# Zero points of the second wave unpacked on chip, row tiles loaded two steps apart, first results stored sooner

## The chip, the cores and the metric

The kernel runs on one core of one Trainium2 chip. The metric is the device time of one execution in microseconds, the median of three runs. The profile shows one further execution; all times of single instructions below are counted from the start of its span.

## What is computed

The input `u` has 2 x 1024 rows of 1024 numbers, 2048 rows in all. The reference is a "macaron": half a feed-forward layer, a state-space convolution along the rows, and half a feed-forward layer again.

```python
x = x + 0.5 * ffn(layernorm(x))
x = x + s4(layernorm(x))
x = x + 0.5 * ffn(layernorm(x))

def ffn(x):                       # 1024 -> 2752 -> 1024
    h = silu(x @ Wg) * (x @ Wu)
    return h @ Wd
# every W is packed in 4 bits, in groups of 128 rows:
W = (w4 - (z4 + 1)) * scale       # z4 (the zero points) is packed as well

def s4(u):                        # one kernel K of length 1024 for all rows
    K = ifft(c * (k00 - k01 * (1 / (1 + k11)) * k10)).real
    return irfft(rfft(u, n=2L) * rfft(K, n=2L))[..., :L] + D * u
```

## The kernel before

**Jobs, stages, steps.** The rows are cut into four blocks of 512. Eight jobs (a block and one of its two feed-forward layers) follow one another, and each has an up stage and a down stage. An up stage has 64 steps: eight "waves" of columns (three pairs of gate and up tiles, 128 columns each, in the first five waves, two pairs in the last three), and in each wave the eight groups of 128 weight rows. A step with three pairs is 12 matmuls of 128x128 weights on 512 rows (L876): the six weight tiles meet the low halves (`xTl`) and the high halves (`xTh`) of the activations. Sums stay in PSUM for the eight steps of a wave; after each step every sum `pg` is multiplied by the ratio of two group scales, on ScalarE or VectorE (L834, L838). After the last step of a wave, ScalarE makes `g` (L912) and VectorE `hf` (L915) of each pair; that frees the pair's two PSUM banks for the next wave. There are eight banks in all. GpSimd then splits `hf` into two halves `h` (L920, L921). A down stage has 44 steps (two halves of the output, 22 groups each) of eight matmuls (L993) into sums `po`, at the end of which `y` is copied out (L834, L838), turned by VectorE (L1052), stored to `yz` (L1058), read back by rows as `yr` (L1063) and added to the block's rows `x` by GpSimd (L1068).

**Weights.** Job 0 makes the weights once. For wave w the packed words `raw` are loaded and shifted into `even` and `raw` (L654), zero points `z` are added (L658), signs are fixed (L661), the bytes are cast to bf16 by ScalarE (L698) and GpSimd (L700), stored to DRAM (`wq`, L706; L642 for the first wave), and each step then loads its tile `w_s` from there (L804). Waves are counted from 0 in the code, so the second wave is wave 1 and its first tile is `w_8`. The zero points of wave 0 are unpacked on chip from `zq_first` (L351 shifts, L360). For the later waves all zero points are unpacked into a table `ztab`, stored to `z_dram` by ScalarE's queue (L380) and loaded per wave by two DMAs on SyncE (L597, `fetch_zeros`).

**The convolution kernel.** In the up stage of job 1 the tables of the state-space part are worked out in 71 pieces spread over the steps (`s4_tables`, `S4_PIECES`). Near the end, VectorE writes the kernel `k` (L1305), GpSimd adds D to one element of it (L1306), SyncE stores it to `k_dram` (L1308) and reads it back as a table `s_rows` with one row shifted per partition (L1325), and TensorE flips it with two matmuls per half (L1330).

**Order.** Each engine runs its instructions in the order of the built program. That order is made by a scheduler, except where the kernel fixes it: `pinned(f, engines)` and `in_order_of_writing` keep what `f` writes behind what was written before on these engines. `at(hooks, s, f)` hangs `f` on step s (s + 0.5: in its middle). A piece of `s4_tables` is kept in order on VectorE alone; GpSimd's chores (`squared`, `most`: L934, L935, the watch over the size of `h`) are kept in order on GpSimd. SyncE issues nearly all DMAs, one after another, and waits at the head of its queue. DMAs that SyncE and ScalarE issue use eight semaphore lanes in turn, and a DMA waits until the earlier one on its lane has landed. At the end of a down stage, `load_x` puts four loads of 512 KB on SyncE (L174) at one step, and `results_out` hangs the turns and stores of the first half's results.

## Time and profile before

| | us |
|---|---|
| three runs | 1948.53, 1948.57, 1949.28 |
| median | 1948.57 |
| the profiled execution, its own time | 1951.13 |
| its span | 1949.1 |
| TensorE busy | 1916.2 (98%) |
| VectorE, ScalarE, GpSimd busy | 1537.9, 1449.7, 1195.3 |
| mean granted TensorE clock | 0.998 |

The profiled execution took 2.56 us more than the median, and 2.0 us of it lie outside the span. TensorE is busy nearly all the time, so a change gains or loses what it takes from, or adds to, TensorE's idle time, and the time in which TensorE runs at less than its clock. Idle times of the other engines count only where TensorE ends up waiting for them.

Some places on the time axis: first up-stage matmul of job 0 at 17.86, its step 8 (the first of the second wave) at 47.16, its down stage from 180.3, up stage of job 1 from 261.04.

### The profile page before, as it was taken

What the parts mean: (1) busy time and instruction counts of PE and PEld (TensorE: products, weight loads), DVE (VectorE), ACT (ScalarE), POOL (GpSimd) and SP (SyncE); (2) the same over time, 40 slices, a digit from 0 to 9 for tenths busy, and PEclk for the clock granted to TensorE, in tenths of its full rate; (3) what the DMA queues carried; (4) which work ended last, traced back from release to release, by engine and by line L of the source; (5) the groups of instructions that cost most, each with busy time, mean ns of one, the idle gap of its engine ahead of it and who ended that gap; (6) DMA issues with size and microseconds to landing.
All of it is one profiled execution on the core that took longest, in us unless ns stands there. A gap on an engine that the chain in (4) does not pass through costs nothing.

```text
span 1949.1 us, 28195 instructions
## 1 busy us (share of the span) xinstructions
PE 1916.2 (98%) x9154; PEld 919.6 (47%) x9154; DVE 1537.9 (79%) x2592; ACT 1449.7 (74%) x2308; POOL 1195.3 (61%) x1314
## 2 busy tenths in 40 slices
PE   6999989999999999999999999999999999999998
PEld 3444434474445544444444444456444564444443
DVE  8888867877877778877887878777877777787787
ACT  7888867738786587787777877874878757777776
POOL 4756959858866681696427960574924858345630
PEclk9999999999999999999999999999999999999999
DMA  6666773345635356644373625443465433663225
GB/s 206 206 201 211 207 239 100 105 126 154 200 110 139 98 149 183 207 123 106 99 239 121 156 72 153 143 118 112 114 195 152 121 101 111 181 197 97 73 70 178
DMA packets 393602, 286.23 MB, mean 147 GB/s; under 512 B 208205, under 2 KB 367254, under 8 KB 393446
## 3 DMA queue, kind: packets, MB, share of 16 engines
q1 hardware_dynamic: 391982, 281.83, 49.9%
q10 hardware_dynamic: 1272, 2.12, 0.3%
q8 instruction: 74, 1.21, 0.3%
q14 instruction: 82, 0.67, 0.1%
q0 software_dynamic: 192, 0.39, 0.1%
HBM read 211.30 MB, written 72.75 MB: 146 GB/s over the span
## 4 chain that ended last, share of the span: by engine, by line
PE 90%; POOL 3%; DVE 2%; DMA 2%; ACT 2%; issue 1%; SPq 0%; ACTq 0%; DVEq 0%; POOLq 0%
PE pg L876 54%; PE po L993 30%; PE pc L1377 4%; PE pb L1377 1%; DVE pg L838 1%; ACT pg L834 1%; POOL most L935 1%; POOL h L921 1%; POOL squared L934 1%; DMA yr<-yz 0%; DMA wd<-wdq 0%; DMA x<-in_L_attn_u_dram 0%; POOL x L1068 0%; DMA z<-z_dram 0%; POOL h L920 0%
## 5 line engine op out<-in xcount | busy, mean ns | idle before, releaser
L834 ACT ACTIVATE pg<-pg,rat 128x512 f32<-128x512 f32 x1356 | 843.1, 661 | 328.4 <-PE pg L876 325.0
L876 PEld LDWEIGHTS <-w 128*128 128x128 bf16 x5504 | 537.6, 98 | 665.6 <-issue 29.8
L838 DVE TENSOR_TENSOR pg<-pg,rat 128x512 f32<-128x512 f32 x1052 | 698.9, 692 | 187.6 <-PE pg L876 182.6
L876 PE MATMUL pg<-xTl,w 128*128 128x512 f16 x2752 | 701.0, 379 | 5.0 <-ACT pg L834 1.7
L876 PE MATMUL pg<-xTh,w 128*128 128x512 f16 x2752 | 698.5, 379 | 5.7 <-DVE pg L838 1.9
L993 PE MATMUL po<-h,wd 128*128 128x512 f16 x2680 | 585.6, 380 | 3.8 <-DMA wd<-wdq 3.1
L834 ACT ACTIVATE po<-po,ratd 128x512 f32<-128x512 f32 x708 | 452.0, 664 | 103.4 <-PE po L993 102.1
L838 DVE TENSOR_TENSOR po<-po,ratd 128x512 f32<-128x512 f32 x572 | 394.3, 693 | 97.6 <-PE po L993 95.9
L993 PEld LDWEIGHTS <-wd 128*128 128x128 bf16 x2740 | 267.8, 98 | 331.6 <-issue 8.9
L920 POOL CAST h<-hf 128x512 f16<-128x512 f32 x168 | 107.4, 641 | 226.1 <-DVE hf L915 225.8
L935 POOL TENSOR_TENSOR most<-most,squared 128x512 f32<-128x512 f32 (+1 forms) x176 | 223.8, 1272 | 8.5
L1068 POOL TENSOR_TENSOR x<-x,yr 128x512 f32<-128x512 f32 x56 | 70.9, 1265 | 236.4 <-DMA yr<-yz 234.1
L921 POOL TENSOR_TENSOR h<-hf,h 128x512 f16<-128x512 f32 x168 | 194.7, 1162 | 10.9
L934 POOL TENSOR_TENSOR squared<-h 128x512 f32<-128x512 f16 x168 | 176.1, 1048 | 4.9
L915 DVE SCALAR_TENSOR_TENSOR hf<-pg,rat,g 128x512 f32<-128x512 f32 x168 | 120.7, 744 | 34.3 <-ACT g L912 28.9
L912 ACT ACTIVATE g<-pg,rat 128x512 f32<-128x512 f32 x168 | 109.9, 685 | 18.8 <-PE pg L876 14.0
L272 POOL TENSOR_SCALAR x<-x,mv,r 128x512 f32<-128x512 f32 x56 | 117.2, 2096 | 0.3
L312 POOL TENSOR_TENSOR xTl<-turned,xTh 128x512 f16<-128x512 f32 x56 | 64.6, 1154 | 3.7
L191 DVE BATCH_NORM_STATS2 stats<-x 128x6 f32<-128x512 f32 x88 | 59.2, 679 | 0.1
L310 POOL CAST xTh<-turned 128x512 f16<-128x512 f32 x56 | 34.1, 609 | 28.2 <-DMA turned<-tz 27.8
L1052 DVE STREAM_TRANSPOSE y<-y 128x256 f32<-128x256 f32 x120 | 50.5, 426 | 0.0
L1371 POOL TENSOR_TENSOR sums<-st 128x384 f32<-128x384 f32 x16 | 15.9, 997 | 55.3 <-PE pb L1377 55.2
(226 smaller groups left out, 866.9 us busy)
## 6 DMA issues: line engine op xcount, KB each, us to landing
w<-wq SPq DMA_DIRECT2D x319, 192.0 KB
wd<-wdq SPq DMA_DIRECT2D x336, 128.0 KB
w<-wq SPq DMA_DIRECT2D x128, 128.0 KB
x<-in_L_attn_u_dram SPq DMA_DIRECT2D x30, 512.0 KB
yz<-y SPq DMA_DIRECT2D x60, 256.0 KB
yr<-yz SPq DMA_DIRECT2D x60, 256.0 KB
tz<-x SPq DMA_DIRECT2D x28, 512.0 KB
turned<-tz SPq DMA_DIRECT2D x112, 128.0 KB
```

Source lines behind the costliest of these rows:

```text
L272: nc.gpsimd.tensor_scalar(part, part, m, r, ALU.subtract, ALU.mult)
L834: nc.scalar.activation(dst, src, AF.Copy, scale=sc)
L838: nc.vector.tensor_tensor(dst, src, sc.to_broadcast(list(dst.shape)), ALU.mult)
L876: product = lambda: nc.tensor.matmul(p, weights, (lo, hi)[k][:, g, :], start=(g == 0 and not done), stop=(g == GK - 1 and done), skip_grou ...
L912: nc.scalar.activation(g, pg, AF.Silu, scale=rat[:, 2 * f, GK - 1 :])
L915: nc.vector.scalar_tensor_tensor(hf, pu, last, g, ALU.mult, ALU.mult)
L920: nc.gpsimd.tensor_copy(hi, hf)
L921: nc.gpsimd.tensor_tensor(lo, hf, hi, ALU.subtract)
L934: chores.append(lambda: nc.gpsimd.tensor_tensor(own, hi, hi, ALU.mult))
L935: chores.append(lambda: nc.gpsimd.tensor_tensor(total, total, own, ALU.add))
L993: nc.tensor.matmul(ps[c], w[:, bass.ts(c, P)], part, start=(f == 0 and k == 0), stop=(f == NF - 1), skip_group_check=True,)
L1377: nc.tensor.matmul(dst, lhsT, rhs, start=start, stop=stop, skip_group_check=True)
```

## The change

The zero points of the second wave are no longer taken from the table. Their packed words are loaded by two more DMAs at the start (`zq_first_1`, one on SyncE after `x_2`, one on ScalarE's queue after `x_3`) and unpacked on VectorE in nine pieces, four before the first turned column block, four after it and one in step 1; the eight zero-point pieces of the table, its last step and its store to `z_dram` move from the start to steps 3 to 4.5 of job 0. The two table loads for wave 1 are gone, those for wave 2 hang on step 5 and no longer on step 2. Shifts, additions and casts of wave 1 hang on earlier steps.

In the down stage of job 0 the four row tiles are loaded at steps 37, 39, 41 and 43, the last row tile to be normalized is turned a little sooner, and the first half's results are turned from step 27.5 on in half steps and stored at steps 33 and 34.

In the state-space part, two ScalarE operations of 1024 columns are cut in halves with pieces between them, two sign changes move from VectorE to GpSimd, and the count of pieces goes from 71 to 74.

```diff
-    def load_x(b, src):
-        x[b] = []
+    def load_row_tile(b, src, t):
+        if t == 0:
+            x[b] = []
+        xt = t4(f"x_{b}_{t}")
+        nc.sync.dma_start(xt, src[t])
+        x[b].append(xt)
...
     def fetch_zeros(w):
...
-        packed[w][1] = z
+        zeros_of[w] = z
...
-    def first_zero_words():
+    def first_zero_words(w):
...
-            nc.vector.tensor_tensor(both, both, z.bitcast(U16), ALU.add)
+            nc.vector.tensor_tensor(both, both, z().bitcast(U16), ALU.add)
...
-            steps = (0.5, 1, 2.5, 3, 3.5) if w == 1 else range(6)
+            steps = (0.5, 1, 1.5, 2, 2.5) if w == 1 else range(6)
...
-            copies = {1: (3, 3, 3.5, 3.5) + (3.5,) * 4, 2: (3, 3, 4, 4, 5.5, 5.5, 6, 6)}
+            copies = {1: (2, 2, 2.5, 2.5) + (3,) * 4, 2: (3, 3, 4, 4, 5.5, 5.5, 6, 6)}
...
-        nc.vector.tensor_scalar(neg, vec[:, 0, :], -1.0, None, ALU.mult)
+        nc.gpsimd.tensor_scalar(neg, vec[:, 0, :], -1.0, None, ALU.mult)
         yield
         dr = t4("s4_dr")
-        nc.scalar.activation(dr, cs, AF.Copy, scale=neg[:, 0:1])
         di = sn
-        nc.scalar.activation(di, sn, AF.Copy, scale=alpha)
-        yield
         halves = [slice(0, 512), slice(512, HID)]
+        for own in halves:
+            nc.scalar.activation(dr[:, own], cs[:, own], AF.Copy, scale=neg[:, 0:1])
+            yield
+            nc.scalar.activation(di[:, own], sn[:, own], AF.Copy, scale=alpha)
+            yield
...
-        nc.vector.tensor_scalar(se[:, 1, :], se[:, 1, :], -1.0, None, mul)
+        nc.gpsimd.tensor_scalar(se[:, 1, :], se[:, 1, :], -1.0, None, mul)
...
-    S4_PIECES = 71
+    S4_PIECES = 74
...
-                    (0, lambda: fetch_zeros(1)),
                     (0, lambda: ask(5)),
...
                     (1, lambda: fetch(2)),
-                    (2, lambda: fetch_zeros(2)),
                     (3, lambda: keep_rest(3, 0)),
+                    (5, lambda: fetch_zeros(2)),
...
+                at(up, 1, pinned(lambda: next(later["zeros"], None), ET.DVE))
                 first_weights(up, dn, at)
+                steps = [(up, s) for s in (3, 3, 3, 3.5, 3.5, 3.5, 4, 4, 4, 4.5)]
+                in_pieces(at, steps, lambda: zero_points_in_pieces(0, later["points"]))
...
-                        turn = ((10.5, 11, 11.5, 12), (17.5, 18, 18.5, 19), (19.5, 24, 24.5, 25), (25.5, 26, 27, 28))[t]
+                        turn = ((10.5, 11, 11.5, 12), (17.5, 18, 18.5, 19), (19.5, 24, 24.5, 25), (25.5, 26, 26.5, 27))[t]
...
-            at(dn, 35 if after else 21, pinned(lambda: load_x(b, rows_of(u, b) if k == 1 else saved(b)), ET.SP))
+            src = rows_of(u, b) if k == 1 else saved(b)
+            if j:
+                at(dn, 35 if after else 21, pinned(lambda src=src: load_x(b, src), ET.SP))
+            for t in range(NT) if j == 0 else ():
+                at(dn, 37 + 2 * t, pinned(lambda t=t, src=src: load_row_tile(b, src, t), ET.SP))
             if j == 0:
-                results_out(at, dn, 0, range(29, 37), (38, 38, 39, 39))
+                results_out(at, dn, 0, [27.5 + i / 2 for i in range(8)], (33, 33, 34, 34))
...
     def start():
-        zq = first_zero_words()
+        zq = first_zero_words(0)
...
             (nc.sync, nc.scalar)[t % 2].dma_start(x[0][t], src)
+        zq_1 = first_zero_words(1)
...
-        points = zero_points_in_pieces(0, zeros)
+        zi_1, z_1 = (t4(f"{a}_w1").bitcast(I32)[:, : width_of(1)] for a in ("zi", "z"))
+        zeros_of[1] = z_1
+        later["zeros"] = unpacked_zeros_in_pieces(z_1, zq_1, zi_1)
+        later["points"] = zeros
         for _ in range(4):
-            next(points)
+            next(later["zeros"])
         first_turn(0)
-        for _ in range(5):
-            next(points)
+        for _ in range(4):
+            next(later["zeros"])
...
-        for _ in points:
-            pass
```

More of the change, by code (lines that the diff above doesn't have):

```diff
@@ L168, in macaron_s4_kernel @@
     ln = {}
+    def load_row_tile(b, src, t):
[4 more added lines that the diff above has]
+        x[b].append(xt)
     def load_x(b, src):
-        x[b] = []
         for t in range(NT):
-            xt = t4(f"x_{b}_{t}")
-            nc.sync.dma_start(xt, src[t])
-            x[b].append(xt)
+            load_row_tile(b, src, t)
     def rows_of(dram, b):
@@ L597, in fetch_zeros @@
             nc.sync.dma_start(z[:, own], src.unsqueeze(1).to_broadcast([GK, 16, hi - lo]))
-        packed[w][1] = z
-    def first_zero_words():
-        n = width_of(0) // 8
-        z = t2("zq_first").bitcast(I32)[:, :n]
-        for queue, (own, i, lo, hi) in zip((nc.sync, nc.scalar), columns(0)):
+        zeros_of[w] = z
+    zeros_of = {}
+    def first_zero_words(w):
+        n = width_of(w) // 8
+        z = t2(f"zq_first_{w}").bitcast(I32)[:, :n]
+        for queue, (own, i, lo, hi) in zip((nc.sync, nc.scalar), columns(w)):
             own = slice(own.start // 8, own.stop // 8)
@@ L664, in split @@
     def split(w):
-        raw, z = packed[w]
+        raw, _ = packed[w]
         even = t4(f"even_{w}").bitcast(I32)[:, : width_of(w)]
-        return signed_bytes(w, raw, even, z, w > 1)
+        return signed_bytes(w, raw, even, lambda: zeros_of[w], w > 1)
     def in_pieces(at, hooks_and_steps, pieces, engines=(ET.DVE,)):
@@ L725, in split_down @@
         both, z = packed[a, rt]
-        return signed_bytes((a, rt), both[:, 0], both[:, 1], z)
+        return signed_bytes((a, rt), both[:, 0], both[:, 1], lambda: z)
     def dequantize_down(a, rt, j):
```

## The prediction

> **What bounds the kernel now.** I read the whole-program shares first (TensorE 98%), then TensorE's waits, then the stretches around each place that the change touches. TensorE's waits are few and have addresses:

> ```profile
> PE pg L876 <- DVE pg L838: 3.3, 12, 0.5
> PE po L993 <- DMA wd<-wdq: 3.1, 1, 3.1
> PE pg L876 <- DMA w<-wq: 2.4, 2, 1.4
> PE pg L876 <- ACT y L834: 0.8, 1, 0.8
> ```

> Columns: total, times, longest. The 3.1 is the end of job 0's down stage, the 2.4 are two weight tiles of the start, and the 0.8 is the boundary to job 1. The time axis of TensorE gives their places, and that of one more instruction which does not wait:

> ```profile
> 29.77 0.82 PE L876 MATMUL pg<-xTh,w 128*128 128x512 f16 x3 [1.35 <-DMA w<-wq]
> 47.16 0.82 PE L876 MATMUL pg<-xTl,w 128*128 128x512 f16 x3 [1.01 <-DMA w<-wq]
> 253.30 2.98 PE L993 MATMUL po<-h,wd 128*128 128x512 f16 x9 [3.10 <-DMA wd<-wdq]
> ...
> 370.17 1.02 PE L1330 MATMUL s_t<-s_rows,s_turn 128*128 128x512 f32 x2
> ```

> Columns: start, length, what, in brackets the idle time before it. L1330 has no bracket: its table `s_rows` landed at 366.55, with 3.4 us to spare (370.17, less 0.19 for its weight load). On GpSimd, the `s_rest` addition that starts this table stands ahead of a run of other work:

> ```profile
> 360.55 0.20 POOL L232 TENSOR_TENSOR r<-f,r 128x4 f32<-128x4 f32 x1
> 360.70 0.18 POOL L1306 TENSOR_TENSOR s_rest<-s_rest 1x1 f32<-1x1 f32 x1
> 360.84 1.26 POOL L935 TENSOR_TENSOR most<-most,squared 128x512 f32<-128x512 f32 x1
> 362.11 2.07 POOL L1703 TENSOR_SCALAR xn<-x,mv,r 128x512 f32<-128x512 f32 x1
> 364.14 0.19 POOL L1314 MEMSET s_turn<- 128x128 f32 x1
> 364.41 0.29 POOL L1315 TENSOR_SCALAR_AFFINE_SELECT s_turn<-s_turn 128x128 f32<-128x128 f32 x1
> 364.71 2.07 POOL L1703 TENSOR_SCALAR xn<-x,mv,r 128x512 f32<-128x512 f32 x1
> 366.74 1.04 POOL L934 TENSOR_TENSOR squared<-h 128x512 f32<-128x512 f16 x1
> 367.86 1.27 POOL L935 TENSOR_TENSOR most<-most,squared 128x512 f32<-128x512 f32 x1
> 369.21 1.04 POOL L934 TENSOR_TENSOR squared<-h 128x512 f32<-128x512 f16 x1
> 370.33 1.26 POOL L935 TENSOR_TENSOR most<-most,squared 128x512 f32<-128x512 f32 x1
> ```

> It is also not idle before: from 351.67, where it waited 1.75 us for `hf` of TensorE's last wave, to 371.59 it works through. Line numbers are those of the old kernel throughout; landings are read from the DMA events of the same trace.

> **Part 1, the new order on GpSimd in job 1 (loss).** With 74 pieces the built order of the changed kernel has the `s_rest` addition behind the last line shown, not ahead of the third. Nothing pins it: the piece is kept in order on VectorE only. The work it now waits for took 360.84 to 371.59, so it runs 371.59 - 360.70 = 10.9 us later. After it, in the old run: store to `k_dram` issued 360.90, landed 362.29, table read issued 362.37, landed 366.55: 5.7 us that stay. The place of L1330 is the same in both orders (before step 39 of job 1). TensorE therefore waits 10.9 - 3.4 = 7.5 us. Ends: 6.6, if the read takes the 3.3 us of the 512 KB `tz` store at 237.29 rather than its 4.18; 9, if GpSimd enters the stretch up to 1.5 us late. The two sign changes given to GpSimd (0.25 to 0.30 us each by L1247, L1189) lie ahead of the 1.75 us of idle time at 351.67, which covers them. SyncE stands at the store until the addition is done (as it did from 357.0 to 360.9); behind it is `w_43`, needed only four steps after L1330, so no second wait.

> After the 3.10 us gap at 250.21, eight matmuls from 254.39 to 257.78 came every 427 ns instead of 216, and the granted clock of 250 to 260 was 0.83; after gaps of 0.96 to 1.35 us none did. The cost is 8 x 0.211 = 1.7 us. A 7.5 us gap is nearest to that row: 1.7 more (0 to 3.4, none or twice that). Sum of part 1: +9.2 (5.5 to 12.4).

> [...]

> **Part 2, the start (loss).** Two DMAs more at the start turn the eight lanes on by two. ScalarE's second `zq` load, which waited for `x_0` (7.30), now waits for `x_2` (9.84). Behind it on ScalarE stand the squares of the layernorm (8.57), then an unbroken chain to the first matmul: 9.84 + 0.5 for the issue - 8.57 = 1.8 us later. The wait for `w_3` (1.35) goes, as the two zero-point loads in front of it do. GpSimd's casts of wave 1's second part (L700, 3.13 us for four) now follow a column block that ScalarE copies only after its own four casts (3.5 us), so wave 1 gains little: stored at 39 to 41, plus 4.3 (the row of a store that ran alone, 55.24 to 59.57), both stores have landed at 43.3 to 45.1, against 44.63. I take X = 44.3 for the issue of `w_8` (44.76 before).

> The zero points of wave 2 now stand on SyncE behind `w_8` and `w_9`. On VectorE their addition (L658, waiting for both loads) stands between the first and the second `hf` of wave 0; before, it stood ahead of all three and ran at 42.08:

> ```profile
> 42.08 0.94 DVE L658 TENSOR_TENSOR even<-even,z 128x1536 uint16<-128x1536 uint16 x1
> ...
> 45.44 2.06 DVE L915 SCALAR_TENSOR_TENSOR hf<-pg,rat,g 128x512 f32<-128x512 f32 x3
> ```

> Queued behind the addition is the second `hf`, and for the bank that it frees waits the ninth matmul of step 8. The same sequence of loads (tile, tile, two zero-point loads) landed 39.94 - 33.30 = 6.64 us after its first issue. So the bank is free at X + 6.64 + 1.0 (L658) + 0.7 (L915) = X + 8.35. Without the wait the matmul would run at X + 2.35 (`w_8`: 44.76 to 47.11) + 8 x 0.216 = X + 4.1. New wait: 4.25 us, and the matmul moves from 48.89 to 52.65: +3.8. The gap is longer than 3.10, so the slow clock again, +1.7. Sum: +5.5. Ends: +1.5 (X = 43.3, loads half a transfer sooner, no slow clock), +7 (X = 45.1, and 0.7 of late rescales).

> **Part 3, the end of job 0's down stage (gain).** Before, four 512 KB loads stood on SyncE ahead of `wd_40` (landed 253.25, wanted 250.21). Now `wd_39` to `wd_43` come first, but behind the four `yz` stores. These issue from 243.80 (0.55 each), so `wd_39` is issued at about 246.1; the transfers before it end at 245.99, the four `yz` take 0.7 each and it 0.35: landed 249.15, wanted at 250.21 - 1.73 = 248.48, a wait of 0.65 (0 to 1.5) that costs no clock. Gain 3.10 + 1.7 - 0.65 = 4.15.

> **Part 4, the boundary and the halves (gain).** Between 263 and 269 TensorE idles 0.20 + 0.20 + 0.80 + 0.38 + 0.39 = 2.0 us, as the copies of `y` come behind three steps of new sums; the new order copies first, and no other boundary shows a gap over 0.2: gain 2.0 (0.5 to 2.5). ScalarE operations of 1.1 to 1.2 us at 283.04 and 284.11 hold rescales up by 0.32 + 0.22 + 0.38; in halves they are as short as a rescale (0.66): gain 0.9 (0 to 0.9). Parts 3 and 4: -7.05 (-2.5 to -8.2).

> **Sum.** 9.2 + 5.5 - 7.05 = +7.65. On the profiled execution 1951.13 + 7.65 = 1958.8; on the median 1948.57 + 7.65 = 1956.2.

> **Rivals.**
> - *The zero-point loads of wave 2 land in time* (chance 0.07). They would have to land by X + 2.4, over 4 us sooner than the row says. For: two loads and a store fewer share the DMA engines there. Against: the first such load, into a nearly empty queue, took 3.3 (23.39 to 26.66). The matmul then runs at X + 4.1 = 48.4 instead of 48.89; total 9.2 - 0.5 - 7.05 = +1.65: 1950.2.
> - *The table read is in time* (0.08). Place: the `s_rest` addition. Not slower if GpSimd reaches it by about 367, so that the wait is under 3.7 and without the slow clock. For: spans on GpSimd are rough. Against: its work there is unbroken, and its only slack is the 1.75 us at 351.67. Price -9.2: 1947.0.
> - *Both waits are absent* (0.07): the written order is not what binds. Then parts 3 and 4 alone: 1941.5, faster.
> - *`yz` ahead of `wd_39` only moves the old stall* (0.1). For: DMA share 0.94 to 0.96 in 240 to 260. Against: 2 MB of loads have moved behind the weights. Price 4.15 back: 1960.4.
> - *The stall at the table runs deeper* (0.1): slow clock for two stretches and GpSimd late, part 1 at 12.4: 1959.4.

> **How the numbers follow.** The forecast has 0.58. A measurement of this kernel tells 0.2% (3.9 us) from no change; slower than 1952.5 are the forecast and the last two rivals, 0.78; within it the first two, 0.15; faster 0.07. The range leaves out the two rarest sides: from the first rival with a little gain more (1949.5) to both upper ends together (1961).

> **What would show it.** In the new profile: a wait of TensorE at L1330 of 6.6 to 9 us, released by the DMA `s_rows`, with GpSimd's `s_rest` addition behind the two `xn`; a wait of 3 to 4.5 us in the middle of step 8, released by VectorE's `hf`, with VectorE idle before its addition on the DMA `z`; the first matmul near 19.7; no wait over 1.5 us for `wd`; no gaps around the first steps of job 1. I am wrong if L1330 waits under 3 us, if VectorE does not stop before that addition, or if the `wd` wait stays.

## The result and the profile after

| | before | after |
|---|---|---|
| median of six runs each, us | 1949.14 (1948.53 to 1951.45) | 1964.51 (1963.55 to 1964.82) |
| profiled execution, us | 1951.13 | 1964.68 |
| its span, us | 1949.1 | 1962.5 |
| mean granted TensorE clock | 0.998 | 0.997 |

The ratio is 1.0076 with an interval of 1.0063 to 1.0089. The changed kernel is slower, by 15.4 us on the medians and 13.4 us between the two spans, where +7.65 was predicted; 1964.51 lies above the stated range, which ended at 1961. The two differences are not the same because the profiled run of the old kernel was 2.0 us slower than its median. Every run takes about 2 us more than its span (1964.68 for 1962.5; 1949.49 for 1947.4 in another run of the old kernel), so these 2.0 us lie inside the old span, and not outside it as is said above; where, no trace shows. The line numbers of the changed kernel are 6 to 8 higher than those of the old one (L876 is now L882, L1330 is L1338); from here on each kernel is quoted with its own.

TensorE's waits of the changed kernel (what waited, what for; total in us, times, longest):

```profile
...
PE pg L882 <- DVE pg L844: 8.9, 13, 3.5
PE s_t L1338 <- DMA s_rows<-k_dram: 8.1, 1, 8.1
PE pg L882 <- DVE hf L921: 3.2, 1, 3.2
...
PE po L999 <- DMA wd<-wdq: 2.2, 2, 1.8
```

Of the rows shown, the second is the predicted wait at the table and the third the predicted wait in the middle of step 8. The old 3.1 us wait for `wd` shrank to 1.8. New in the first row is its longest wait, 3.5 us, where it was 0.5 before. TensorE's time axis gives the four places (start, length, what, in brackets the idle time before it):

```profile
52.60 0.38 PE L882 MATMUL pg<-xTh,w 128*128 128x512 f16 x1 [3.23 <-DVE hf L921]
...
255.91 7.08 PE L999 MATMUL po<-h,wd 128*128 128x512 f16 x32 [1.79 <-DMA wd<-wdq]
...
281.61 0.59 PE L882 MATMUL pg<-xTh,w 128*128 128x512 f16 x2 [3.51 <-DVE pg L844]
...
381.75 2.05 PE L1338 MATMUL s_t<-s_rows,s_turn 128*128 128x512 f32 x2 [8.05 <-DMA s_rows<-k_dram]
```

Both traces hold 9154 matmuls in the same order (but for 80, where one with the low halves and one with the high halves trade places), so the start of each can be compared with the start of its counterpart before. That difference is a ledger of the change; it moves at these places:

| stretch (time after) | predicted | measured | shift reached |
|---|---|---|---|
| start, to step 9 of job 0 | +5.5 | +5.2 | +5.2 |
| end of job 0's down stage, 239 to 262 | -4.15 | -2.6 | +2.6 |
| boundary to job 1, 264 to 269 | -2.0 | -3.0 | -0.4 |
| job 1, 276 to 292 | -0.9 | **+4.7** | +4.3 |
| job 1, to 354 | 0 | -0.9 | +3.4 |
| the flip of the table, 373 to 387 | +9.2 | +10.2 | +13.5 |
| all that follows | 0 | -0.2 | +13.4 |

After the boundary the changed kernel was ahead of the old one by 0.4 us. The misses of the other rows cancel out. The fourth has the other sign, and its 5.6 us (+4.7 for -0.9) are about as much as the whole prediction fell short on the traces (13.4 for 7.65).

**The unpredicted wait.** VectorE in that place:

```profile
273.82 1.30 DVE L844 TENSOR_TENSOR pg<-pg,rat 128x512 f32<-128x512 f32 x2
279.35 0.15 DVE L1120 TENSOR_SCALAR s_vc<-s_vc 128x1 f32<-128x1 f32 x1 [4.23 <-DMA s_vc<-in_L_attn_log_step_dram]
...
280.87 0.69 DVE L844 TENSOR_TENSOR pg<-pg,rat 128x512 f32<-128x512 f32 x1
```

L1120 is the first state-space operation of job 1. It takes 0.15 us on 128 numbers, but VectorE stood for 4.23 us ahead of it until `log_step`, one number written to 128 partitions, was there, and behind it stood the rescale of 280.87, for which TensorE waited 3.51 us. SyncE issued that load as the twelfth and last of a row of small loads:

```profile
266.53 0.48 SPq L1106 DMA_DIRECT2D s_vc<-in_L_attn_Lambda_ri_dram  x1
...
274.02 0.43 SPq L1111 DMA_DIRECT2D s_vc<-in_L_attn_log_step_dram  x1
```

Before, the same row began 1.1 us after the first matmul of job 1, and L1120's counterpart, L1114, ran without a wait. SyncE and VectorE of the old kernel:

```profile
262.16 0.48 SPq L1100 DMA_DIRECT2D s_vc<-in_L_attn_Lambda_ri_dram  x1
...
269.26 0.43 SPq L1105 DMA_DIRECT2D s_vc<-in_L_attn_log_step_dram  x1
```

```profile
275.42 0.15 DVE L1114 TENSOR_SCALAR s_vc<-s_vc 128x1 f32<-128x1 f32 x1
```

After, job 1 began at 263.69, the row 2.8 us behind that, and use followed 5.33 us after the issue. Two things met: the loads came 2.1 us later in the job (10.33 us after its first matmul, 8.22 before), and VectorE, with the stalls of the boundary gone, was ready for that operation 3 us sooner in the job (11.4 us after its first matmul, 14.4 before).

**The clock.** Stretches of the changed kernel (stretch, its length, busy time and instructions of TensorE, weight loads, VectorE, ScalarE, GpSimd; granted clock, DMA share, GB/s):

```profile
45.00:55.00 10.00, 6.77 (x32) 2.91 (x30) 6.43 (x10) 5.67 (x10) 4.51 (x6) 1.00 0.84 251
...
280.00:290.00 10.00, 7.82 (x28) 3.10 (x28) 7.09 (x22) 7.07 (x12) 5.00 (x5) 0.83 0.96 316
...
380.00:390.00 10.00, 8.26 (x26) 3.42 (x27) 3.74 (x6) 3.49 (x6) 3.35 (x4) 0.72 0.30 105
```

The eighth column is the clock. The gap of 3.23 us at 49 cost none, the gap of 3.51 at 278 brought it to 0.83 in that stretch, and the gap of 8.05 at 374 to 0.72.

### The profile page after: what moved, and what is told of

It is laid out like the page before. It is cut to its first block, busy times and chain, and to the rows that moved or that the text cites. A ratio compares the mean times of both kernels' runs of the same rounds, so it can differ in the third digit from the quotient of the medians.

```text
span 1962.5 us, 28207 instructions
## 1 busy us (share of the span) xinstructions
PE 1917.1 (98%) x9154; PEld 920.2 (47%) x9154; DVE 1541.2 (79%) x2599; ACT 1451.2 (74%) x2310; POOL 1198.4 (61%) x1316
## 3 DMA queue, kind: packets, MB, share of 16 engines
q10 hardware_dynamic: 1408, 2.14, 0.3%
## 4 chain that ended last, share of the span: by engine, by line
PE 91%; DVE 3%; DMA 2%; ACT 1%; POOL 1%; issue 1%; SPq 0%; DVEq 0%; POOLq 0%; ACTq 0%
PE pg L882 56%; PE po L999 30%; PE pc L1385 4%; PE pb L1385 1%; DVE pg L844 1%; ACT pg L840 1%; DMA x<-in_L_attn_u_dram 1%; DMA wd<-wdq 0%; DMA z<-z_dram 0%; DMA s_rows<-k_dram 0%; DMA s_vc<-in_L_attn_log_step_dram 0%; DVE hf L921 0%; POOL xn L1711 0%; DMA zq<-n_L_ffn_gate_qzeros_dram 0%; POOL most L941 0%
## 5 line engine op out<-in xcount | busy, mean ns | idle before, releaser
L882 PEld LDWEIGHTS <-w 128*128 128x128 bf16 x5504 | 538.5, 98 | 670.5 <-issue 39.2
L882 PE MATMUL pg<-xTh,w 128*128 128x512 f16 x2752 | 699.2, 379 | 10.2 <-DVE pg L844 5.7
L882 PE MATMUL pg<-xTl,w 128*128 128x512 f16 x2752 | 702.2, 380 | 4.0 <-DVE pg L844 3.2
```

The lines of the kernel that those rows point to most:

```text
L882: product = lambda: nc.tensor.matmul(p, weights, (lo, hi)[k][:, g, :], start=(g == 0 and not done), stop=(g == GK - 1 and done), skip_grou ...
```

## The experiments

Each ratio is taken to runs of the kernel before on the same chip; their medians were 1949.3 to 1949.7. Where "the ledger" is named, it is the comparison by matmul described above.

**Is the flip late because of GpSimd's order?** The addition of D is given to VectorE, where it lies in the fixed order of the pieces:

```diff
-        nc.gpsimd.tensor_tensor(k[:1, 0:1], k[:1, 0:1], d, ALU.add)
+        nc.vector.tensor_tensor(k[:1, 0:1], k[:1, 0:1], d, ALU.add)
```

> The changed kernel with one operation moved: D is added to the convolution kernel by VectorE, directly behind the copy that it needs, and no longer by GpSimd behind two normalizations and five chores. Theory (late addition): the wait of 8.05 us at the flip of the table goes, and the 2 us of slow clock after it; 1964.5 - 10 = 1954.5, no wait of TensorE on s_rows. Rival (GpSimd is late as a whole, its s_turn or its copies bind next): a wait of over 3 us stays at the flip, and the time stays above 1959.

1953.75 (1952.67 to 1955.56, 10 runs), ratio 1.0023 [1.0014, 1.0033]. The flip on TensorE's time axis in this kernel has no bracket:

```profile
371.95 1.02 PE L1338 MATMUL s_t<-s_rows,s_turn 128*128 128x512 f32 x2
```

The span is 11.8 us shorter than that of the changed kernel: 10.2 at the flip by the ledger, 1.3 at the start (whose wait was 2.09 here). The place of one addition on a 1x1 operand costs 10 us of the 13.

**Which of the edits around the flip turned the order?** The state-space edits are taken back (pieces of 71, both ScalarE operations whole, both sign changes on VectorE):

```diff
-        nc.gpsimd.tensor_scalar(neg, vec[:, 0, :], -1.0, None, ALU.mult)
+        nc.vector.tensor_scalar(neg, vec[:, 0, :], -1.0, None, ALU.mult)
...
-    S4_PIECES = 74
+    S4_PIECES = 71
```

> The changed kernel with the state-space edits undone (whole 1024-column operations on ScalarE, both sign changes on VectorE, 71 pieces). Theory (it is these edits that put the addition of D behind the chores): the wait at the flip goes (-10), the 0.9 us of short waits near 283 and the 1 us near 350 come back; 1964.5 - 10 + 2 = 1956.5. The wait near 278 on log_step stays, since it comes from the row loads. Rival (the wait at the flip comes from the earlier start of job 1): it stays, and the time is 1964 or more.

1954.94 (1953.22 to 1955.32, 8 runs), ratio 1.0024 [1.0014, 1.0035]. The addition stands ahead of GpSimd's chores again and the wait at the flip is gone. The wait near 278 stays (3.85 us), so these edits do not make it. Which of them turns the order was not separated. Between 276 and 292 this kernel loses 0.5 us more than the changed one, 0.34 of it in the longer wait, and the old kernel's short waits of 0.32, 0.22 and 0.38 us appear in neither. So the 0.9 us predicted for the halves can't be read from this pair.

**The start.** The whole start as it was before, all else as in the changed kernel:

```diff
-        zq = first_zero_words(0)
+        zq = first_zero_words()
...
+                    (0, lambda: fetch_zeros(1)),
...
-            steps = (0.5, 1, 1.5, 2, 2.5) if w == 1 else range(6)
+            steps = (0.5, 1, 2.5, 3, 3.5) if w == 1 else range(6)
```

> The changed kernel with its start undone (zero points of the second wave from the table again, before's order of the start), the rest as changed. Theory (the start costs 5.2 us by itself): no wait in the middle of step 8, the old short waits on w_3, on a rescale and on w_8 return, and all that follows is shifted: 1964.5 - 5.2 = 1959.3, with the waits near 278 and at the flip unchanged (3.5 and 8). Rival (what the start loses is slack that later waits would take anyway): the wait near 278 grows by 3 us or more, and the time stays above 1962.

1959.83 (1956.92 to 1960.49, 4 runs), ratio 1.0044 [1.0029, 1.006]; span 4.9 us shorter than the changed kernel's. The waits near 278 (3.47) and at the flip (7.83) are where they were. The start costs its predicted 5 us, and none of the later waits comes from it.

**Does the wait of the start only move?** Wave 2's additions of zero points are hung up to 2.5 steps later, behind the three `hf`. The casts stay where they are and now come before the addition, so in this kernel the weights of wave 2 lack their zero points.

```diff
-            steps = (0.5, 1, 1.5, 2, 2.5) if w == 1 else range(6)
+            steps = (0.5, 1, 1.5, 2, 2.5) if w == 1 else (0, 1, 4.5, 5, 5.5, 6) if w == 2 else range(6)
```

> The changed kernel with the zero-point additions of wave 2 hung 2.5 steps later, so that all three hf of wave 0 stand ahead of them on VectorE. Theory (VectorE waits for the wave's zero points between the first and the second hf): the 3.2 us wait in the middle of step 8 goes, with about 1 us of late rescales behind it; 1964.5 - 4.3 = 1960.2. Rival (it only moves: wave 2 is stored later, and its first tile is late at step 16): a wait of 2 to 4 us on a tile at step 16, 1963 to 1965.

1964.54 (1963.13 to 1964.64, 4 runs), ratio 1.0077 [1.006, 1.0094]: no gain. VectorE (first two lines) and TensorE of this kernel:

```profile
47.15 2.22 DVE L921 SCALAR_TENSOR_TENSOR hf<-pg,rat,g 128x512 f32<-128x512 f32 x3
52.44 1.76 DVE L664 TENSOR_TENSOR even<-even,z 128x1536 uint16<-128x1536 uint16 x1 [3.07 <-DMA z<-z_dram]
```

```profile
54.86 0.97 PE L882 MATMUL pg<-xTh,w 128*128 128x512 f16 x3 [2.01 <-DVE pg L844]
```

The three `hf` run through and the ninth matmul of step 8 does not wait, but VectorE still stops at the addition, and the next thing queued behind it, a rescale, stops TensorE. Which instruction waits changed; the late load and an engine that stands at it did not.

**The row tiles.** All four loads at step 35 again, the sooner results kept:

```diff
-            if j:
-                at(dn, 35 if after else 21, pinned(lambda src=src: load_x(b, src), ET.SP))
-            for t in range(NT) if j == 0 else ():
-                at(dn, 37 + 2 * t, pinned(lambda t=t, src=src: load_row_tile(b, src, t), ET.SP))
+            at(dn, 35 if after else 21, pinned(lambda src=src: load_x(b, src), ET.SP))
```

> The changed kernel with the four row tiles of job 0's down stage loaded together at step 35 again; everything else as changed, the stores of the first results still ahead of wd_39. Theory (the row tiles, put between the weight tiles of job 1, hold SyncE and so the loads of the state-space part): these loads are issued about 4 us earlier against TensorE, the 3.5 us wait near 278 goes (-5.5 with its slow clock), and the old wait for wd_40 comes back with 3 to 4 us and its slow clock in place of 1.8 (+3 to +4): 1961 to 1962.5. Rival (the loads are late for another reason, the earlier stores of yz): the wait near 278 stays above 2.5 us, and the time is 1967 or more.

1969.11 (1968.92 to 1971.26, 4 runs), ratio 1.0099 [1.0084, 1.0115], the slowest of all. TensorE's waits in it:

```profile
PE po L999 <- DMA wd<-wdq: 6.8, 2, 4.8
...
PE pg L882 <- DVE s_vc L1121: 2.9, 1, 2.9
```

With four `yz` stores and four row tiles ahead of the weights, the `wd` wait is 6.8 us instead of 2.2. The wait of job 1 stays as well (2.9), though `log_step` is issued only 6.49 us into the job (10.33 in the changed kernel): the built order has put L1120 behind six rescales instead of ten, and VectorE stands there for 3.52 us. So the wait does not need the row tiles to be apart.

**The results.** The first results are turned and stored at the old steps, the row tiles stay apart:

```diff
-                results_out(at, dn, 0, [27.5 + i / 2 for i in range(8)], (33, 33, 34, 34))
+                results_out(at, dn, 0, range(29, 37), (38, 38, 39, 39))
```

> The changed kernel with the first results turned and stored at the old steps (29 to 36, then 38 and 39), so that wd_39 to wd_43 stand ahead of all yz stores. Theory (the four yz stores ahead of wd_39 cost the two waits on wd): no wait on wd over 0.3 us, -2.4. The stores now stand between the row tiles and hold SyncE a little longer, so the wait near 278 stays at 3.5 or grows by up to 1: 1962 to 1963. Rival (the rows come back later and GpSimd, which is on the way to the table, gets later): the wait at the flip grows by over 2 us, 1964.5 or more.

1961.57 (1960.6 to 1961.85, 4 runs), ratio 1.0056 [1.004, 1.0071]. The time is 0.4 us under the expected 1962 to 1963; its way there was not the expected one. The longest `wd` wait is down to 0.6, 2.5 us are lost at the boundary, and the wait near 278 is gone too (by the ledger against the changed kernel, 5.9 us gained between 270 and 286). Of that, 2.7 are lost again by 354, most in a wait of 1.60 us for a rescale at 342. VectorE in this kernel:

```profile
277.40 1.30 DVE L844 TENSOR_TENSOR pg<-pg,rat 128x512 f32<-128x512 f32 x2 [1.29 <-PE pg L882]
...
279.52 0.15 DVE L1120 TENSOR_SCALAR s_vc<-s_vc 128x1 f32<-128x1 f32 x1
```

`log_step` is issued at 274.13 here, no sooner in the job than in the changed kernel, and used 5.39 us later. But L1120 now has thirteen rescales of job 1 ahead of it instead of ten, so VectorE comes to it when the load is there, if only just: 5.39 us is as long as the load took where VectorE waited for it.

**Is it the load of `log_step`?** Two kernels. In one it is the first of the row of small loads, in the other it is loaded at step 20 of the down stage into a tile of its own:

```diff
+        ls = tiny()
+        nc.sync.dma_start(ls, log_step.partition_broadcast(P))
         for o in (0, NST):
...
-        ls = tiny()
-        nc.sync.dma_start(ls, log_step.partition_broadcast(P))
```

> The changed kernel with the load of log_step first among the loads of the state-space part and no longer behind eleven others. Theory (VectorE stands for 4.2 us at the first operation on log_step, ahead of a rescale that TensorE needs, because that load is issued 4.8 us later than before): the load is issued some 6.8 us earlier, the 3.5 us wait of TensorE near 278 and the slow clock after it go, 1964.5 - 5.5 = 1959. Rival (the whole queue of SyncE is late, the next load takes the place): VectorE or ScalarE stops at another of these loads, TensorE still waits over 2 us near 280, at least 1963.

```diff
-        ls = tiny()
-        nc.sync.dma_start(ls, log_step.partition_broadcast(P))
+        ls = log_t
...
+            if j == 0:
+                at(dn, 20, pinned(lambda: nc.sync.dma_start(log_t, log_step.partition_broadcast(P)), ET.SP))
```

> The changed kernel with log_step loaded at step 20 of job 0's down stage into a tile of its own, so that VectorE's first state-space operation waits for no load; all other loads as changed. Theory (what TensorE gains at the end of job 0 and at the boundary is handed back at this one load): no wait of VectorE on log_step, no wait of TensorE over 0.7 us between 262 and 290, and the slow clock there goes too: 1964.5 - 5.7 = 1958.8. Rival (the next loads of the same queue, the rows for sine and cosine or the poles, take its place): a wait of 2 us or more between 275 and 290 stays, at least 1962.

Loaded first: 1961.0 (1959.57 to 1962.55, 4 runs), ratio 1.0064 [1.0047, 1.0081]. The 3.51 us gap is gone, but the built order now puts L1120 behind four rescales and VectorE still waits 1.84 us at 269.91, which gives TensorE gaps of 1.23, 0.53 and 0.46. Loaded early: 1963.44 (1962.64 to 1965.61, 4 runs), ratio 1.0079 [1.0062, 1.0096]. VectorE does not wait for `log_step` at all, and between 262 and 290 TensorE has a single gap over 0.3 us, 0.93 at 276. Against the changed kernel, TensorE gains 3.9 us between 258 and 286. The total missed its expectation, since by 258 it stood 3.2 us later than the changed kernel: the `wd` wait grew from 1.79 to 3.08, with a slow clock behind it (0.64 from 258 to 262). The four `yz` stores were issued up to 253.29 instead of 252.17; that the added load turned the eight semaphore lanes (semaphores 100 to 107 in the traces of before and after) on by one is a possible reason and was not tested.

The place of that operation and of its load, from the traces of these kernels and of the one below:

| kernel | first results | load issued, us into job 1 | rescales of VectorE ahead of it | VectorE's wait |
|---|---|---|---|---|
| before | old steps | 8.22 | 10 | none |
| after | sooner | 10.33 | 10 | 4.23 |
| start undone | sooner | 10.25 | 10 | 4.18 |
| state-space edits undone | sooner | 10.75 | 10 | 4.57 |
| row tiles together | sooner | 6.49 | 6 | 3.52 |
| `log_step` first | sooner | 2.63 | 4 | 1.84 |
| results late | old steps | 11.92 | 13 | none |
| row tiles apart alone | old steps | 11.49 | 13 | none |

In every kernel with the sooner results and the load in its row, VectorE waits (in those not listed, 3.76 with D on VectorE, 3.33 with wave 2 late, 2.35 in the first of the last three kernels); with the old result steps it waits 0.20 us at most. The row tiles two steps apart move the load some 3 us later into the job, and the operation goes three rescales later with it; the sooner results bring the operation back to the tenth and the load hardly. The sooner results without the row tiles apart are enough for a wait (3.52), the row tiles apart without the sooner results are not. Why the scheduler places the operation so was not examined.

**Row tiles apart alone**, everything else as before (but for the last row tile to be normalized, which is turned a little sooner as in the change):

```diff
+            src = rows_of(u, b) if k == 1 else saved(b)
+            if j:
+                at(dn, 35 if after else 21, pinned(lambda src=src: load_x(b, src), ET.SP))
+            for t in range(NT) if j == 0 else ():
+                at(dn, 37 + 2 * t, pinned(lambda t=t, src=src: load_row_tile(b, src, t), ET.SP))
```

> The kernel before with one part of the change alone: row tiles of job 0's down stage loaded two steps apart (and the last tile turned a step sooner). Theory (the four loads in front of wd_40 are what TensorE waited for at 250): the wait of 3.1 us on wd and its slow clock go (-4.8), at most 1 us of it comes back where yz or the state-space loads are later: 1949.3 - 4 = 1945. Rival (the gain is handed back within job 1, at log_step or at the table): 1948 to 1950.

1949.68 (1948.47 to 1952.08, 10 runs), ratio 1.0004 [0.9994, 1.0013]: no change, by way of a gain and a loss. No wait for `wd` is left. TensorE is 5.2 us ahead after the boundary and 6.7 at 287 of the old axis, and 4.9 of that go by 346, at places where the old kernel had smaller gaps or none. Why these rescales come late was not traced:

```profile
283.33 0.38 PE L880 MATMUL pg<-xTl,w 128*128 128x512 f16 x1 [0.97 <-ACT pg L838]
286.62 0.38 PE L880 MATMUL pg<-xTh,w 128*128 128x512 f16 x1 [0.96 <-DVE pg L842]
294.31 0.38 PE L880 MATMUL pg<-xTl,w 128*128 128x512 f16 x1 [1.06 <-DVE pg L842]
...
343.70 0.59 PE L880 MATMUL pg<-xTl,w 128*128 128x512 f16 x2 [0.83 <-DVE pg L842]
```

**What is left when the losing parts are dropped.** Three kernels with the start of before, the row tiles apart, the halves, and D added by VectorE. The first has the sooner results and `log_step` loaded first:

> The kernel before with its own start, plus the row tiles two steps apart, the sooner stores and the halves of the change, plus D added by VectorE and log_step loaded first. Theory (three separate losses, of which the start is one, and a gain at the end of job 0's down stage and the boundary): what is left of the losses is a wait of about 1.2 us near 270; 1964.5 - 10.5 (flip) - 4 (log_step) - 5.2 (start) = 1944.8, about 4 us faster than before. Rival (the gains were small and the measured differences hang together): no faster than 1948.

The second has the old result steps and `log_step` first, the third the old result steps and `log_step` last. Against the first:

```diff
-                results_out(at, dn, 0, [27.5 + i / 2 for i in range(8)], (33, 33, 34, 34))
+                results_out(at, dn, 0, range(29, 37), (38, 38, 39, 39))
```

> The best of the parts, first try: the kernel before with row tiles two steps apart and halves, D added by VectorE, log_step loaded first, and the first results stored at the old steps. Theory: no wait on wd over 0.7, none at the flip, one of up to 1.7 us on log_step; 1947.5 (the same with the sooner stores) - 1.8 = 1945.7. Rival (the later stores hold the rows and GpSimd up): a new wait of 1 to 2 us near 340, 1947 or more.

> The same as b3_yzlate with log_step loaded last as before; the built order then puts VectorE's first state-space operation behind 13 rescales of job 1 and not behind 8. Theory (the wait on log_step is the distance between that load and that place): no wait on it, 1945. Rival (the pieces are only later, and the table with them): a wait at the flip of 1 us or more, 1947.

| kernel | median, us | runs | ratio |
|---|---|---|---|
| results sooner, `log_step` first | 1947.45 (1945.61 to 1949.48) | 11 | 0.9987 [0.9978, 0.9997] |
| results as before, `log_step` first | 1945.93 (1944.67 to 1950.96) | 10 | 0.9988 [0.9978, 0.9997] |
| results as before, `log_step` last | 1946.19 (1944.26 to 1949.28) | 10 | 0.9987 [0.9978, 0.9997] |

All three beat both kernels, by some 0.12% against the one before. The intervals end just under 1, and they do not tell the three apart. In the first, waits of 1.77 for `wd` and 1.74 behind `log_step` stay. In the second, TensorE's longest gap from 255 to 345 is 0.92, and `log_step` is used 7.8 us after its issue, with room to spare. By the ledger, row tiles apart alone are left with 1.8 us of their gain at 350, the second and third kernel with 4.8 and 5.1 (0.6 of the 5.1 from its start, which is that of the old kernel). These two have the state-space edits and D on VectorE, which the other has not; what each of them is worth there was not taken apart.

## Why the prediction was right in direction and wrong in size

**Direction and main mechanism: right.** The waits that were named, at the table, in the middle of step 8 and for `wd`, stand in the trace where they were put, each with the releaser that was named; the last is 0.3 us longer than the 1.5 allowed for it. Three figures of the prediction do not follow from its terms: the low end of part 1 is 6.6 (its least wait, no slow clock) and not 5.5, that of parts 3 and 4 is 3.10 + 1.7 - 1.5 + 0.5 = 3.8 and not 2.5, and 41 + 4.3 is 45.3 and not 45.1. None of them enters its sum.

**Part 1, the flip: right, 1.0 too small.** GpSimd works through as predicted and the addition comes behind the last chore:

```profile
365.19 2.08 POOL L1711 TENSOR_SCALAR xn<-x,mv,r 128x512 f32<-128x512 f32 x1
...
373.42 1.26 POOL L941 TENSOR_TENSOR most<-most,squared 128x512 f32<-128x512 f32 x1
374.64 0.18 POOL L1314 TENSOR_TENSOR s_rest<-s_rest 1x1 f32<-1x1 f32 x1
```

Less the 3.4 us by which all of TensorE was late by then, 374.64 is 371.3, that is 10.6 us after the old 360.70, where 10.9 was predicted. The trip through `k_dram` took 6.9 us from the addition to the use, not 5.85 (1.07 more); 10.6 + 1.07 - 3.4 = 8.2 is the shift of 8.22 there. The slow clock after it (0.50 from 378.71 to 385.54) took 1.95, not 1.7. Without the addition on GpSimd 10.2 us came back.

**Part 2, the start: right in sum (5.2 for 5.5), in part by luck, as its terms were others.** VectorE stopped at the addition, between the first and the second `hf`:

```profile
46.73 0.75 DVE L921 SCALAR_TENSOR_TENSOR hf<-pg,rat,g 128x512 f32<-128x512 f32 x1
50.93 0.96 DVE L664 TENSOR_TENSOR even<-even,z 128x1536 uint16<-128x1536 uint16 x1 [3.44 <-DMA z<-z_dram]
51.80 0.75 DVE L921 SCALAR_TENSOR_TENSOR hf<-pg,rat,g 128x512 f32<-128x512 f32 x1
```

The wait of TensorE was 3.23, not 4.25, and had no slow clock behind it (1.00 from 51.04 to 54.45). In their place 1.5 us were lost right after, as rescales queued behind the stopped VectorE came late (0.91 and 0.54 by the ledger); the prediction had left these to its upper end. They are not added to a slow clock: in the kernel with the late results the gap was 3.29 with eight slow matmuls behind it, and at the end of step 8 it stood within 0.1 us of the changed kernel. The first matmuls lost 1.7 us as said, and up to step 8 all but 0.3 of it came back. The size of this wait varies: 2.1 to 3.3 us in the kernels here that share this start.

**Part 3, the end of the down stage: right place, gain 2.6 instead of 4.15.** The failed step is "0.55 each" for the issue of the four `yz` stores:

```profile
249.04 3.13 SPq L1064 DMA_DIRECT2D yz<-y  x4
252.27 4.24 SPq L817 DMA_DIRECT2D wd<-wdq  x6
```

They took 3.1 us instead of 2.2, so `wd_39` was issued at 252.27 and came late by 1.79 us, not 0.65, and 0.5 were lost at 239 besides. Leaving the results at their old steps made that wait 0.6.

**Part 4, the boundary: gain 3.0 instead of 2.0.** The copies of `y` do come first. Where the row tiles alone move and the results keep their old steps, the down stage's end gains 5.1 and the boundary 0.6. So the sooner results cost 2.5 at `wd` and bring 2.4 at the boundary; what stays of them is the wait behind `log_step`. (Against the changed kernel with the results late, they cost only 1.0 at `wd`.)

**Where it failed.** "Parts 3 and 4: -7.05" was carried to the end of the job as if nothing behind it were near its limit. In its place the ledger shows -2.6, -3.0 and +4.7, together -0.9. The prediction followed the moved loads past the weights in the queue of SyncE, but not the twelve small loads that stand in the same queue behind the last row tiles, nor who waits for the last of them. They were listed nowhere, since before L1114 did not wait for its load: 6.16 us lay between issue and use, where 4.9 to 5.4 are needed (issue to use wherever VectorE waited), so the slack was only some 0.8 us. The load came 2.1 later in the job and VectorE 3 us sooner; less the slack that is the wait of 4.23. It cost TensorE the 3.51 us and some 1.7 of slow clock behind them (0.50 from 283.14 to 286.55). The kernel that loads `log_step` early shows the cause: without that wait the 3.51 us gap is gone and 3.9 us come back. Whether the halves' 0.9 was there no run shows by itself.

**Rivals.** That `yz` ahead of `wd_39` only moves the old stall was half true (1.8 of 3.1 us, but without its slow clock). The stall at the table ran 1.0 us deeper, not the 3.2 of the last rival. Those in which the zero points or the table come in time are excluded by the two waits. None had the mechanism that decided the size: a gain of TensorE that is spent waiting for the next load.

**Open.** The wait for the zero points of wave 2 was taken away only by undoing the whole start; which part of the start makes it was not separated. The longer `wd` wait of the kernel that loads `log_step` early has no tested cause. The ledger's -0.9 up to 354 comes where the old kernel had two short waits (0.32 at 349.8, 0.22 at 350.4) that the changed one has not; they are gone with the state-space edits undone as well (its shift falls from +5.3 at 346 to +4.5 at 350), so those edits are not the cause.

## What to carry to other kernels

When a change frees the engine that sets the time, list the next loads behind it with their slack from issue to use, those without a wait too: here a load of one number to 128 partitions, with 0.8 us of slack, swallowed 4 us of gain. When a piece may move on one engine because its order is fixed only on another, read its new place in the built order, and put a tiny step that starts a round trip through DRAM on the engine where its order is fixed. And test the parts alone as well as together: the sooner results gained nothing that could be measured here, and without them and without the new start, with D added by VectorE, the rest was faster than the kernel before.

## What the runs showed of the hardware

**A gap of 2.0 to 3.3 us cost clock in some places and runs and not in others.** Counting the matmuls that followed one another at 0.43 us instead of 0.216 after each gap of TensorE between 25 and 450 us, in all traces of this study:

| gaps, us | a slow stretch after them | none |
|---|---|---|
| 1.0 to 1.9 | none | all |
| 2.0 to 3.3 | 2.04, 2.14, 2.54, 2.57, 2.62, 2.91, 3.04, 3.08, 3.10, 3.29 | 2.00, 2.00, 2.01, 2.09, 2.21, 2.65, 3.23 |
| 3.4 to 4.8 | 3.47, 3.51, 3.85, 4.81 | none |

At the same place, the middle of step 8, a gap of 3.23 cost nothing and one of 3.29 eight slow matmuls, and 2.14 cost seven where 2.21 cost none. What such a stretch looks like, from the kernel that loads `log_step` early (six of these matmuls take 1.46 us at full clock):

```profile
51.91 0.38 PE L882 MATMUL pg<-xTh,w 128*128 128x512 f16 x1 [2.54 <-DVE hf L921]
52.13 2.19 PE L882 MATMUL pg<-xTl,w 128*128 128x512 f16 x6
```

```profile
47.62:51.04 3.42, 1.75 (x9) 0.68 (x7) 0.11 (x1) 2.22 (x4) 1.70 (x2) 1.00 0.84 262
51.04:54.45 3.41, 1.85 (x9) 0.87 (x9) 3.41 (x5) 0.66 (x1) 1.83 (x3) 1.00 0.96 284
```

```profile
48.96:52.37 3.41, 0.30 (x2) 0.02 (x1) 1.50 (x2) 1.37 (x3) 0.33 (x1) 1.00 1.01 305
52.37:55.78 3.41, 3.23 (x8) 1.13 (x8) 3.41 (x6) 0.66 (x1) 3.22 (x4) 0.50 0.87 225
```

The gap of 3.23 was split in two, 1.67 and 1.56 us of idle time in two steps, and the clock stayed; of the gap of 3.29, 3.11 us fell into one step, and the next ran at half clock. So it was throughout: between 25 and 450 us of all fourteen traces, the clock never fell after a full-clock step in which TensorE was idle for 1.84 us or less, and fell after each of the 21 with 2.04 us or more (in the old kernel after one of 2.31 us, in the changed one after two of 2.46 and 3.41, and not after one of 1.71). Counted from the start of the span, the grid lay elsewhere in each of these traces (a step begins at 47.62 in the changed kernel and at 48.96 in the one with the results late), so a gap between some 2 and 4 us (an estimate: 4 is twice 2.04, and no split of more than that in two leaves both parts under 2.04) cost 0 or up to 1.7 us (a step of 3.41 us at a clock of 0.50) by where it fell. The prediction put the slow clock into its sums from 3.10 us on, with ends without it.

**A small load was not a quick one here.** `log_step`, one number written to 128 partitions, took 4.9 to 5.4 us from its issue to its use wherever it was waited for, as long as the 5.3 us from the issue of the read of `s_rows` at 376.26 to its use, and each load of its row held SyncE for 0.4 to 0.6 us.
